# A two-layer cross-attention kernel: its start reordered, and the context of later batches loaded in 32 by 32 blocks and turned by VectorE

## The chip, the cores and the metric

The kernel runs on one core of one Trainium2 chip. The metric is device time in microseconds (us) of one execution. Everything is float32. The engines are named as in the profile: PE is TensorE (matmul), PEld its weight loads, DVE is VectorE, ACT is ScalarE, POOL is GpSimd, SP is the engine that issues nearly all DMAs.

## The reference, cut to what matters

There are 4 batches; x has 1024 rows of 512, the context 1024 rows of 384.

```python
# layer 0, 16 heads of 64
h = layernorm(x, gamma, beta)
Q, K, V = h @ Wq, context @ Wk, context @ Wv            # each 1024 x 1024 per batch
attn = softmax(Q K^T) * 64 ** -0.5
x = x + (attn @ V) @ Wo + bo
# layer 1, 16 heads of 32
xn = x * rsqrt(mean(x * x) + eps) * norm_w
q = xn @ wq;  k, v = split(context @ wkv)
q, k = rotate(q), rotate(k)                              # rotary position
q, k = q / |q|, k / |k|
attn = softmax(q k^T * sqrt(32))
out = x + (attn @ v) @ wout
```

Both layers multiply the context with weights along its 384 features. A matmul of PE contracts over partitions, so the kernel needs the context turned over: features in partitions, rows along the free axis.

## The kernel before, in words

**Stages.** The batches run one after the other, and each has three stages. Attention 0 works through 8 pairs of heads in 8 steps each (`Attention0.step`): scores on PE (L453), the negated maximum on DVE (L478), the exponential on ACT (L479), scaling on POOL (L484), a 32 by 32 block turn on DVE (L487), and 16 DMAs for every two steps that regroup the blocks (L498, tile eT), after which PE multiplies with the values (L514). Between the attentions the second layer's first queries and keys are made. Attention 1 has two halves (8 heads each) of 32 steps (`Attention1.step`): a block is one group of 4 heads and 256 queries, with four steps of key tiles, kk = 0 to 3. A step has 32 score matmuls (L692), two exponentials of 128x1024 (L702), the product with the values of the step before (L741), filling work, and additions on DVE that collect the sums of the exponentials (L711, L713, L715). The buffer of the exponentials, e, has two places (kk % 2), so the exponentials of a step wait until the additions and the product of the step two before have read theirs. Once a block PE multiplies the sums with ones (L775), and DVE inverts and divides (L760 to L768).

**Filling work.** All other work is cut into units, pairs of a cost and a function. `Units.fill(us)` is called once a step and issues units from the front of the list while it owes time; a unit of cost 0 is issued along with its neighbours. So the order of the list is the order in which the instructions enter the engines' queues, and every engine works strictly through its own queue. SP does so as well: it runs ahead of the others until a DMA must wait for its destination to be free, and all DMAs behind it then wait too. During the second half of attention 1 the units are the beginning of the next batch (`prepare_units(b + 1)`, `order(adds)`): weights and context loaded, context turned, x rows loaded, their mean and variance taken on DVE (`norms[h]["stats"]`, L251 and L252), normalised on DVE (`apply`, L268), turned on PE (`turn`, L283), and keys, queries and values of the first two pairs projected (L172). Among them lie the output additions of the batch that ends (`other`, two matmuls of PE and one addition of DVE, L332, for each of 8 tiles).

**The context.** `context_units` loads 8 tiles of 128 rows (L217), and turns them on PE: for each half of the rows and each 128 features, four 128x128 transposes into one PSUM bank (L226, tile ptc), then a copy by ACT (L144) into the turned context ctxT (cT in the profile). The row tiles have four buffers, ctxT has one, which lives from here to the last projection of values in the first half of attention 1.

**The start of batch 0.** The same units in an order of their own: `loads` names the DMAs in their order on SP, `first` is issued before the first step of attention 0, `rest` is handed out over its first steps.

**PSUM.** Scores have two tiles of two banks; four banks (in attention 1 three) serve everything else through `bank` and `free`.

Of the kernel before, what the change touches and what calls it, by code (L numbers as in the profile page):

```python
# [38 lines left out]
P = 128  # L39
# [69 lines left out]
def xattn_kernel(ctx: ExitStack, tc: tile.TileContext, a: dict, out: bass.AP):  # L109
# [28 lines left out]
    def free(pp, late=0.5):  # L138

        which["reads"] += 1  # L140
        read[held.pop(id(pp))[1]] = work.clock + late + 1e-6 * which["reads"]

    def evac(dst, src):
        nc.scalar.copy(dst, src)  # L144


    ident = const.tile([P, P], F32, name="ident")
    make_identity(nc, ident)
    ones = const.tile([P, HD1], F32, name="ones")
# [57 lines left out]
    def context_units(b, ct):  # L207

        raws = {}

        def load(h):
            for t in range(4 * h, 4 * h + 4):
                if b == 0 and h:
                    raws[t] = sb.tile([P, S], F32, tag="vals", bufs=4, name=f"c_{b}_{t}")[:, :DC]
                else:
                    raws[t] = sb.tile([P, DC], F32, tag="row", bufs=4, name=f"c_{b}_{t}")
                nc.sync.dma_start(raws[t], c[b, t * P : (t + 1) * P, :])  # L217

        def turn_over(h, k):
            if k == 0:  # L220
                if h == 0:
                    both = sb.tile([P, NC_, S], F32, tag="ctxT", bufs=1, name=f"cT_{b}")
                    ct.extend([both[:, :, :512], both[:, :, 512:]])
            pp = bank(f"ptc_{b}_{h}_{k}")
            for t in range(4):
                nc.tensor.transpose(pp[:, t * P : (t + 1) * P], raws[4 * h + t][:, k * P : (k + 1) * P], ident)  # L226
            evac(ct[h][:, k, :], pp)
            free(pp)

        return [  # L230
            {
                "load": [(0.0, lambda h=h: load(h))],
                "turn": [(0.45, lambda h=h, k=k: turn_over(h, k)) for k in range(NC_)],
            }
            for h in range(2)
        ]
# [424 lines left out]
    class Attention1:  # L661
# [17 lines left out]
        def step(self, half, g, qb, kk, kT, qT, v, o, us):  # L679
            n = f"{self.b}_{half}_{g}_{qb}_{kk}"  # L680
            self.n += kk == 0
            if kk == 1:
                self.add_up()
            if kk == 2 and self.late is not None:
                self.late(False)
            sc = [score(f"s1_{n}_{u}", (P, 2, 2, WQ)) for u in range(2)]
            for c in range(2):
                for j in range(4):
                    rr = slice(j * HD1, (j + 1) * HD1)
                    k = 2 * kk + c  # L690
                    for part in range(0, P, HD0):
                        nc.tensor.matmul(  # L692
                            sc[j // 2][part : part + HD0, j % 2, c, :],
                            kT[rr, g, k * P + part : k * P + part + HD0],
                            qT[rr, g, qb * WQ : (qb + 1) * WQ],
                            start=True,
                            stop=True,
                        )
            es = []
            for u in range(2):  # L700
                e = self.e[:, kk % 2, u]
                nc.scalar.activation(e, sc[u], AF.Exp, scale=float(np.sqrt(np.float32(HD1))))  # L702
                es.append(e)
            self.finish()
            self.last = (half, g, qb, kk, v, es, o, self.n % 2, self.lone)
            self.u.fill(us)

            acc, end = self.both[:, self.n % 2], self.both[:, 3]
            into = acc if kk == 0 else end if kk == NT // 2 - 1 else self.both[:, 2]
            for u in range(2):  # L710
                nc.vector.tensor_add(into[:, 2 * u : 2 * u + 2, :], es[u][:, :, 0, :], es[u][:, :, 1, :])  # L711
            if 0 < kk < NT // 2 - 1:
                nc.vector.tensor_add(acc, acc, into)  # L713
            if kk == NT // 2 - 1 and self.lone:
                nc.vector.tensor_add(acc, acc, end)  # L715
# [101 lines left out]
    def flat(lists):  # L817
        return [u for lst in lists for u in lst]

    def prepare_units(b):  # L820
# [4 lines left out]
        def load(names="kqv"):  # L825
            w[0] = pair_load(b, 0, names, w.get(0))
# [22 lines left out]

        st["project"] = lambda p: flat(project(p).values())  # L850
        st["rows"] = begin_rows_of
        cts = context_units(b, st["ct"])
        norms = norm_units(b, 0, st["hT"], load_rows(b))

        def order(other):

            pairs = [project(p) for p in range(2)]
            turned = [join(*norms[h]["turn"][:2]) + join(*norms[h]["turn"][2:]) for h in range(2)]
            n = len(other)

            def some(i):
                return flat(other[n * i // 6 : n * (i + 1) // 6])

            if b == 0:
                loads = [[(0.0, lambda: load("k"))], cts[0]["load"], cts[1]["load"], norms[0]["load"]]
                loads += [[(0.0, columns_load), (0.0, lambda: load("qv"))]]
                loads += [norms[1]["load"], pairs[0]["begin"], [(0.0, constants_load)]]
                first = cts[0]["turn"] + norms[0]["stats"] + pairs[0]["k"][:NC_] + norms[0]["apply"]
                first += cts[1]["turn"] + pairs[0]["k"][NC_:] + norms[1]["stats"]
                first += norms[0]["turn"] + pairs[0]["q"][:NQ] + norms[1]["apply"]  # L870
                rest = pairs[0]["v"][:4] + norms[1]["turn"] + pairs[0]["v"][4:] + pairs[0]["q"][NQ:]
                later = flat([pairs[1][c] for c in ("begin", "k", "q", "v")])
                return flat(loads) + first, rest, later
            return flat(
                [
                    [(0.0, load)] + cts[0]["load"] + some(0) + join(*cts[0]["turn"][:2]) + cts[0]["turn"][2:],
                    cts[1]["load"] + some(1) + join(*cts[1]["turn"][:2]) + cts[1]["turn"][2:],
                    norms[0]["load"] + some(2) + norms[0]["stats"] + pairs[0]["begin"] + pairs[0]["k"],
                    norms[0]["apply"] + some(3) + turned[0],
                    norms[1]["load"] + pairs[0]["v"] + norms[1]["stats"] + some(4),  # L880
                    norms[1]["apply"] + some(5) + turned[1] + pairs[0]["q"],
                    pairs[1]["begin"] + pairs[1]["k"] + pairs[1]["q"],
                ]
            ), pairs[1]["v"]
# [18 lines left out]
    for b in range(B):  # L903
# [14 lines left out]
        for p in range(NPAIR):  # L918
            later = 17.3 * (p == 0)
            other = []  # L920
            if p in by_rows:
# [258 lines left out]
```

## Time and profile before

| | |
|---|---|
| time, median of 3 runs | 2797.65 us (2794.89 to 2800.26) |
| the profiled execution, own time | 2795.07 us |
| its span, first to last instruction | 2793.1 us |
| PE busy | 2771.9 us (99%) |
| DVE busy | 2202.7 us (79%) |
| ACT busy | 1436.9 us (51%) |
| POOL busy | 952.9 us (34%) |
| DMA | 349.90 MB in 177616 packets |
| PE transposes of context (ptc) | 96 in all, 24 a batch |
| ACT copies into cT | 24, median 608 ns |

The profile is that of one execution; times in it are counted from the first instruction of the span. The 2.0 us around the span belong to the execution's time. A row of a group or of the order of time names start, length, engine, line, operation, output and input tiles, shapes, the number of instructions, and in brackets how long the engine was idle before and what ended that. A busy PE is not PE at its peak, since matmuls are pipelined and their ends are modelled.

### The profile page before, as it was taken

To read this page: it belongs to the slowest core of one execution; us is meant where nothing else is said; L and a number is where in the kernel's file an instruction comes from. 1 tells how busy PE (TensorE), PEld (TensorE's weight loads), DVE (VectorE), ACT (ScalarE), POOL (GpSimd) and SP (SyncE) were. 2 spreads that over 40 slices of the span, in tenths; PEclk is the share of its full clock that TensorE was granted. 3 is DMA by queue.
4 is the path that set the end of the run, shared out by engine and by line. 5 is a ranking of instruction groups with operands and counts; after the bars stand their busy time and mean duration, and the time that the engine had idled before them with its cause. 6 is when DMAs were issued, how large, how long until landed. Compare 5 with 4: busy or idle time off the path is not lost.

```text
span 2793.1 us, 82844 instructions
## 1 busy us (share of the span) xinstructions
PE 2771.9 (99%) x35344; PEld 1388.0 (50%) x35344; DVE 2202.7 (79%) x3140; ACT 1436.9 (51%) x2323; POOL 952.9 (34%) x776
## 2 busy tenths in 40 slices
PE   9999999999999999999999999999999999999999
PEld 4444445555444444554554444455445444445543
DVE  5677786888777778698877777869887777886987
ACT  4444443766544444476654444446664444444665
POOL 2343354430234335442023433444202343443410
PEclk9999999999999999999999999999999999999999
DMA  5788776010388877601048888750104887774000
GB/s 143 176 197 189 184 167 165 24 38 27 74 206 193 191 187 164 148 23 38 27 96 202 196 188 189 158 133 24 38 27 116 203 195 185 184 162 117 3 3 32
DMA packets 177616, 349.90 MB, mean 125 GB/s; under 512 B 37600, under 2 KB 93152, under 8 KB 177248
## 3 DMA queue, kind: packets, MB, share of 16 engines
q1 hardware_dynamic: 176848, 344.42, 51.9%
q8 instruction: 278, 4.55, 0.7%
q14 instruction: 90, 0.74, 0.1%
q10 hardware_dynamic: 400, 0.20, 0.0%
HBM read 67.64 MB, written 8.39 MB: 27 GB/s over the span
## 4 chain that ended last, share of the span: by engine, by line
PE 79%; DVE 2%; ACT 2%; issue 1%; POOL 1%; SPq 1%; DMA 0%; DVEq 0%; ACTq 0%
PE s L453 13%; PE av L514 13%; PE s L692 9%; PE av L741 8%; PE pv L172 7%; PE po L172 6%; PE pqT L194 4%; PE po L194 4%; PE q_p L172 4%; PE pkT L194 3%; PE k_p L172 3%; PE pqT L172 1%; PE pkT L172 1%; ACT e L702 1%; PE pth L283 1%
## 5 line engine op out<-in xcount | busy, mean ns | idle before, releaser
L478 DVE TENSOR_REDUCE m<-s 128x1 f32<-128x1024 f32 x512 | 602.9, 1220 | 357.0 <-PE s L453 354.0
L702 ACT ACTIVATE e<-s 128x1024 f32<-128x1024 f32 x512 | 496.8, 1022 | 279.1 <-PE s L692 274.3
L479 ACT ACTIVATE e<-s,m 128x1024 f32<-128x1024 f32 x256 | 283.1, 1110 | 465.2 <-DVE m L478 274.0
L484 POOL TENSOR_SCALAR raw<-raw,li 128x1024 f32<-128x1024 f32 x256 | 287.2, 1122 | 685.1 <-DVE li L483 677.2
L453 PE MATMUL s<-qk 64*64 64x512 f32 x4096 | 514.7, 598 | 2.2 <-ACT e L479 0.9
L479 ACT ACTIVATE raw<-s,m 128x1024 f32<-128x1024 f32 x256 | 285.4, 1115 | 367.5 <-DVE m L478 364.3
L514 PE MATMUL av<-eT,v 128*64 128x256 f32 x4096 | 470.1, 382 | 0.5 <-DMA eT<-e 0.5
L484 POOL TENSOR_SCALAR e<-e,li 128x1024 f32<-128x1024 f32 x256 | 287.4, 1124 | 472.5 <-DVE li L483 270.2
L514 PEld LDWEIGHTS av<-eT,v 128*64 128x64 f32 x4096 | 284.2, 137 | 227.6 <-issue 63.9
L711 DVE TENSOR_TENSOR both<-e 128x512 f32<-128x512 f32 x512 | 342.5, 698 | 67.1 <-ACT e L702 64.4
L487 DVE STREAM_TRANSPOSE e<-e 128x1024 f32<-128x1024 f32 x256 | 310.0, 1229 | 0.3
L487 DVE STREAM_TRANSPOSE e<-raw 128x1024 f32<-128x1024 f32 x256 | 309.9, 1228 | 0.0
L692 PE MATMUL s<-q,k 32*64 32x256 f32 x8192 | 299.2, 387 | 3.9 <-ACT e L702 2.6
L453 PEld LDWEIGHTS s<-qk 64*64 64x64 f32 x4096 | 151.2, 132 | 252.6 <-issue 198.0
L692 PEld LDWEIGHTS s<-q,k 32*64 32x64 f32 x8192 | 156.4, 131 | 158.0 <-ACT e L702 72.4
L172 PE MATMUL pv<-wv,cT 128*64 128x128 f32 (+1 forms) x3360 | 189.1, 273 | 1.4 <-ACT k L590 1.4
L172 PEld LDWEIGHTS pv<-wv,cT 128*64 128x64 f32 (+1 forms) x3360 | 173.8, 132 | 31.1 <-issue 14.6
L194 PE MATMUL pqT<-hT,w 64*64 64x512 f32 x1408 | 161.0, 589 | 0.0
L713 DVE TENSOR_TENSOR both<-both 128x1024 f32<-128x1024 f32 x128 | 156.8, 1225 | 4.4
L741 PE MATMUL av<-e,v 128*32 128x256 f32 x2048 | 137.1, 385 | 0.0
L741 PE MATMUL av<-e,rest 128*32 128x256 f32 x2048 | 136.9, 385 | 0.0
L332 DVE TENSOR_TENSOR x<-x,po 128x512 f32<-128x512 f32 x112 | 74.9, 680 | 67.5 <-PE po L172 67.4
(101 smaller groups left out, 3084.7 us busy)
## 6 DMA issues: line engine op xcount, KB each, us to landing
eT<-e SPq DMA_DIRECT2D x2048, 128.0 KB, 2.4
xr<-in_x_dram SPq DMA_DIRECT2D x32, 256.0 KB, 4.0
w<-in_Wq_dram SPq DMA_DIRECT2D x32, 256.0 KB, 3.2
x<-in_x_dram SPq DMA_DIRECT2D x32, 256.0 KB, 2.9
wo<-in_Wo_dram SPq DMA_DIRECT2D x16, 512.0 KB, 4.3
out_dram<-x SPq DMA_DIRECT2D x32, 256.0 KB, 2.5
c<-in_ctx_dram SPq DMA_DIRECT2D x32, 192.0 KB, 3.7
wv<-in_Wv_dram SPq DMA_DIRECT2D x32, 192.0 KB, 3.4
```

The lines of the kernel that those rows point to most:

```text
L172: nc.tensor.matmul(o[rr], lhsT[:, rr], rhs, start=start, stop=stop)
L194: nc.tensor.matmul(o["pp"][cc], o["lhsT"](k)[rr, cc], o["rhs"](k)[rr], start=first and k == 0, stop=not first and k == n - 1,)
L453: nc.tensor.matmul(sc[j][part : part + HD0, kb * 512 : (kb + 1) * 512], pr["qT"][r[j], i * P + part : i * P + part + HD0], pr["kT"][r[j], ...
L478: nc.vector.tensor_reduce(m[:, j : j + 1], sc[j], AX.X, ALU.max, negate=True)
L479: nc.scalar.activation(e[j], sc[j].rearrange("p (g s) -> p g s", g=4), AF.Exp, bias=m[:, j : j + 1], accum_out=l[:, j : j + 1])
L484: nc.gpsimd.tensor_scalar(e[j], e[j], li[:, j : j + 1], HD0**-0.5, ALU.mult, ALU.mult)
L487: self.turn = [lambda j=j: nc.vector.transpose(self.e[:, :, i % BQ * 2 + j, :], e[j]) for j in range(2)]
L514: nc.tensor.matmul(av[r[j], :W].rearrange("p (t a i) -> p t a i", t=BQ, a=4), pr["v"][:, k, r[j]], eT[:, j, :, :, k * 32 : (k + 1) * 32], ...
L692: nc.tensor.matmul(sc[j // 2][part : part + HD0, j % 2, c, :], kT[rr, g, k * P + part : k * P + part + HD0], qT[rr, g, qb * WQ : (qb + 1) ...
L702: nc.scalar.activation(e, sc[u], AF.Exp, scale=float(np.sqrt(np.float32(HD1))))
L711: nc.vector.tensor_add(into[:, 2 * u : 2 * u + 2, :], es[u][:, :, 0, :], es[u][:, :, 1, :])
L741: nc.tensor.matmul(self.av[rr, 0, :], v[g][:, 2 * kk + c, rr], es[j // 2][:, j % 2, c, :], start=first and c == 0, stop=end and c == 1,)
```

## The change

1. Six matmuls on a tile of zeros are issued at the very start, before any data is there.
2. In batch 0 the context is turned tile by tile (three transposes for each arriving tile, into three banks at once) instead of by features. The second half of its tiles uses a score tile for two of its banks. The loads, the values and the second half's turns are reordered.
3. In batches 1 to 3 PE no longer turns the context. Twelve DMAs load it straight into ctxT, each for 32 features of one group of 128: the piece of 32 rows by 32 features that belongs at partitions g*32 and columns n*32 is written there unturned, in runs of 32 numbers (128 bytes). DVE then turns the 32 by 32 blocks in place, in six instructions of 128x512, which stand between the output additions, the statistics and the normalisation of the next batch. All output additions come ahead of the first projection.
4. The two first additions of a step, one for each exponential, become one of twice the size, except in the last step of a block in the very last half.
5. In batch 0 two projections of values move from the end of attention 0 to pair 2.

```diff
+    still = const.tile([P, P], F32, name="still")
+    nc.vector.memset(still, 0.0)
+    idle = bank("idle")
+    for _ in range(6):
+        nc.tensor.matmul(idle[:, :P], still, still, start=True, stop=True)
+    free(idle)
...
+        def turn_tile(t):
+            h = t // 4
...
+            for k in range(NC_):
+                nc.tensor.transpose(wide[h][k][:, t % 4 * P : (t % 4 + 1) * P], raws[t][:, k * P : (k + 1) * P], ident)
+            if t % 4 == 3:
+                for k, pp in enumerate(wide[h]):
+                    evac(ct[h][:, k, :], pp)
...
+    def context_blocks(b, ct):
+
+        def load():
+            both = sb.tile([P, NC_, S], F32, tag="ctxT", bufs=1, name=f"cT_{b}")
+            ct.extend([both[:, :, :512], both[:, :, 512:]])
+            rows = c[b].rearrange("(n i) (k g f) -> k g i n f", i=32, g=4, f=32)
+            for k in range(NC_):
+                for g in range(4):
+                    to = both[32 * g : 32 * (g + 1), k].rearrange("p (n f) -> p n f", f=32)
+                    nc.sync.dma_start(to, rows[k, g])
+
+        def turn_over(h, k):
+            nc.vector.transpose(ct[h][:, k, :], ct[h][:, k, :])
...
-            for u in range(2):
-                nc.vector.tensor_add(into[:, 2 * u : 2 * u + 2, :], es[u][:, :, 0, :], es[u][:, :, 1, :])
+            both = self.e[:, kk % 2].rearrange("p u j c q -> p (u j) c q")
+            if self.lone or kk < NT // 2 - 1:
+                nc.vector.tensor_add(into, both[:, :, 0, :], both[:, :, 1, :])
...
-        cts = context_units(b, st["ct"])
+        cts = context_units(b, st["ct"]) if b == 0 else context_blocks(b, st["ct"])
...
             if b == 0:
-                loads = [[(0.0, lambda: load("k"))], cts[0]["load"], cts[1]["load"], norms[0]["load"]]
-                loads += [[(0.0, columns_load), (0.0, lambda: load("qv"))]]
+                loads = [[(0.0, lambda: load("k"))], cts[0]["load"], cts[1]["load"], [(0.0, lambda: load("v"))]]
+                loads += [norms[0]["load"], [(0.0, lambda: load("q")), (0.0, columns_load)]]
                 loads += [norms[1]["load"], pairs[0]["begin"], [(0.0, constants_load)]]
-                first = cts[0]["turn"] + norms[0]["stats"] + pairs[0]["k"][:NC_] + norms[0]["apply"]
-                first += cts[1]["turn"] + pairs[0]["k"][NC_:] + norms[1]["stats"]
+                c0, c1 = cts[0]["tiles"], cts[1]["tiles"]
+                first = c0 + norms[0]["stats"] + c1[:1] + pairs[0]["k"][:NC_] + norms[0]["apply"]
+                first += c1[1:] + pairs[0]["v"][:4] + pairs[0]["k"][NC_:] + norms[1]["stats"]
                 first += norms[0]["turn"] + pairs[0]["q"][:NQ] + norms[1]["apply"]
-                rest = pairs[0]["v"][:4] + norms[1]["turn"] + pairs[0]["v"][4:] + pairs[0]["q"][NQ:]
+                first += pairs[0]["v"][4:6] + norms[1]["turn"]
+                rest = pairs[0]["v"][6:] + pairs[0]["q"][NQ:]
...
+            turns = cts[0]["turn"] + cts[1]["turn"]
             return flat(
                 [
-                    [(0.0, load)] + cts[0]["load"] + some(0) + join(*cts[0]["turn"][:2]) + cts[0]["turn"][2:],
-                    cts[1]["load"] + some(1) + join(*cts[1]["turn"][:2]) + cts[1]["turn"][2:],
-                    norms[0]["load"] + some(2) + norms[0]["stats"] + pairs[0]["begin"] + pairs[0]["k"],
-                    norms[0]["apply"] + some(3) + turned[0],
-                    norms[1]["load"] + pairs[0]["v"] + norms[1]["stats"] + some(4),
-                    norms[1]["apply"] + some(5) + turned[1] + pairs[0]["q"],
+                    [(0.0, load)] + cts[0]["load"] + norms[0]["load"],
+                    flat(other[:3]) + turns[:1] + other[3] + norms[0]["stats"] + other[4] + turns[1:2],
+                    other[5] + turns[2:3] + other[6] + turns[3:4] + norms[0]["apply"] + other[7] + turns[4:],
+                    pairs[0]["begin"] + pairs[0]["k"] + turned[0],
+                    norms[1]["load"] + pairs[0]["v"][:4] + norms[1]["stats"] + pairs[0]["v"][4:],
+                    norms[1]["apply"] + turned[1][:1] + pairs[0]["q"][:NQ] + turned[1][1:] + pairs[0]["q"][NQ:],
                     pairs[1]["begin"] + pairs[1]["k"] + pairs[1]["q"],
                 ]
             ), pairs[1]["v"]
...
-                several = [4, 4, 2, 2] if p == 0 else [0, 0, 2, 2] if b == 0 and p == 2 else [2, 2, 2, 2]
+                several = [4, 4, 2, 2] if p == 0 else [0, 2, 2, 2] if b == 0 and p == 2 else [2, 2, 2, 2]
```

More of the change, by code (lines that the diff above doesn't have):

```diff
@@ L228, in turn_over @@
             free(pp)
+        wide = {}
+        def turn_tile(t):
+            h = t // 4
+            if t == 0:
+                both = sb.tile([P, NC_, S], F32, tag="ctxT", bufs=1, name=f"cT_{b}")
+                ct.extend([both[:, :, :512], both[:, :, 512:]])
+                wide[0] = [bank(f"ptc_{b}_0_{k}") for k in range(NC_)]
+            elif t == 4:
+                two = score(f"ptc_{b}_1")
+                wide[1] = [two[:, :512], two[:, 512:], bank(f"ptc_{b}_1_2")]
+            for k in range(NC_):
[3 more added lines that the diff above has]
+                    evac(ct[h][:, k, :], pp)
+                    if id(pp) in held:
+                        free(pp)
         return [
@@ L233, in context_units @@
                 "turn": [(0.45, lambda h=h, k=k: turn_over(h, k)) for k in range(NC_)],
+                "tiles": [(0.33, lambda t=t: turn_tile(t)) for t in range(4 * h, 4 * h + 4)],
+            }
+            for h in range(2)
+        ]
+    def context_blocks(b, ct):
+        def load():
+            both = sb.tile([P, NC_, S], F32, tag="ctxT", bufs=1, name=f"cT_{b}")
+            ct.extend([both[:, :, :512], both[:, :, 512:]])
+            rows = c[b].rearrange("(n i) (k g f) -> k g i n f", i=32, g=4, f=32)
[5 more added lines that the diff above has]
+            nc.vector.transpose(ct[h][:, k, :], ct[h][:, k, :])
+        return [
+            {
+                "load": [(0.0, load)] if h == 0 else [],
+                "turn": [(0.0, lambda h=h, k=k: turn_over(h, k)) for k in range(NC_)],
             }
@@ L709, in step @@
             into = acc if kk == 0 else end if kk == NT // 2 - 1 else self.both[:, 2]
-            for u in range(2):
-                nc.vector.tensor_add(into[:, 2 * u : 2 * u + 2, :], es[u][:, :, 0, :], es[u][:, :, 1, :])
+            both = self.e[:, kk % 2].rearrange("p u j c q -> p (u j) c q")
+            if self.lone or kk < NT // 2 - 1:
+                nc.vector.tensor_add(into, both[:, :, 0, :], both[:, :, 1, :])
+            else:
+                for u in range(2):
+                    part = slice(2 * u, 2 * u + 2)
+                    nc.vector.tensor_add(into[:, part], both[:, part, 0, :], both[:, part, 1, :])
             if 0 < kk < NT // 2 - 1:
@@ L858, in order @@
             turned = [join(*norms[h]["turn"][:2]) + join(*norms[h]["turn"][2:]) for h in range(2)]
-            n = len(other)
-            def some(i):
-                return flat(other[n * i // 6 : n * (i + 1) // 6])
             if b == 0:
-                loads = [[(0.0, lambda: load("k"))], cts[0]["load"], cts[1]["load"], norms[0]["load"]]
-                loads += [[(0.0, columns_load), (0.0, lambda: load("qv"))]]
+                loads = [[(0.0, lambda: load("k"))], cts[0]["load"], cts[1]["load"], [(0.0, lambda: load("v"))]]
```

## The prediction

> **What bounds the kernel now.** I read the page's busy shares first.
>
> ```profile
> PE 2771.9 (99%) x35344; PEld 1388.0 (50%) x35344; DVE 2202.7 (79%) x3140; ACT 1436.9 (51%) x2323; POOL 952.9 (34%) x776
> ```
>
> TensorE (PE) has work for all but 21.2 us of the 2793.1 us span, so time is won by taking work off PE or filling its few gaps, and lost wherever PE is made to wait. Next, the longest waits of PE itself (total us, times, longest):
>
> ```profile
> PE ptc L226 <- DMA c<-in_ctx_dram: 4.8, 3, 3.9
> ...
> PE sum L775 <- DVE both L715: 1.3, 3, 0.4
> ```
>
> The first is the start of the run, the second the end of a batch, where PE needs VectorE's (DVE's) last addition. Now the stretches the change touches: PE, PEld, DVE, ACT, POOL busy us, then clock, DMA share and GB/s. The first two rows are the start (the first scores begin at 22.44); the other five are the second half of batch 0's second attention, in which the next batch's context is turned.
>
> ```profile
> 0.00:9.40 9.40, 4.59 (x16) 2.79 (x18) 0.15 (x1) 3.04 (x4) 0.81 (x8) 1.00 0.82 264
> 9.40:22.44 13.04, 12.35 (x69) 5.43 (x65) 9.90 (x24) 6.09 (x10) 2.43 (x4) 1.00 0.73 232
> ```
>
> ```profile
> 601.60:717.00 115.40, 115.35 (x2129) 55.74 (x2132) 93.57 (x149) 77.99 (x98) 3.08 (x4) 1.00 0.13 39
> 601.60:611.00 9.40, 9.35 (x165) 4.75 (x172) 6.90 (x12) 6.91 (x11) 0.00 (x0) 1.00 0.14 44
> 611.00:621.00 10.00, 10.00 (x180) 4.92 (x172) 5.98 (x9) 7.75 (x10) 0.00 (x0) 1.00 0.42 132
> 621.00:631.00 10.00, 10.00 (x188) 4.39 (x182) 9.38 (x20) 4.95 (x6) 0.00 (x0) 1.00 0.27 83
> 631.00:641.00 10.00, 10.00 (x180) 4.14 (x176) 9.83 (x18) 6.35 (x8) 1.87 (x2) 1.00 0.01 2
> ```
>
> PE is full there, but DVE is nearly so from 621 to 641. Last, the order of time (start, length, engine, line): the transposes of context at the start and in that stretch, and what PE does right after them.
>
> ```profile
> 6.21 2.18 PE L226 MATMUL ptc<-ident,c 128*128 128x128 f32 x9 [0.29 <-DMA c<-in_ctx_dram]
> ...
> 12.02 1.53 PE L226 MATMUL ptc<-ident,c 128*128 128x128 f32 x12
> ```
>
> ```profile
> 607.40 1.53 PE L226 MATMUL ptc<-ident,c 128*128 128x128 f32 x12
> ...
> 608.98 1.07 PE L172 MATMUL po<-wo,o 128*32 128x512 f32 x8
> ...
> 615.58 1.53 PE L226 MATMUL ptc<-ident,c 128*128 128x128 f32 x12
> ...
> 617.04 0.66 PEld L692 LDWEIGHTS s<-q,k 32*64 32x64 f32 x32 [0.17 <-ACT cT L144]
> ```
>
> **Part 1, the start.** Until 22.44 us PE is idle 5.5 us (22.44 less 4.59 and 12.35), and its early work is slow: nine transposes in 2.18 us are 0.24 each, twelve later ones in 1.53 are 0.13. The change runs six matmuls on zeros ahead of the first context tile (3.92), turns the context tile by tile as it lands, and puts values and the second half's turns before the first scores. Laid out by the rows: first-half keys at about 7.7 instead of 8.3, and at full pace; then nine transposes (1.2), four values (2.84 for 48 matmuls at 24.31) and the second-half keys (2.79) end at 17.3 without a gap. The normalised rows are ready at 16.75: the wv load is moved ahead of the x rows and shifts the statistics (9.25 before) by 0.8 us for its 192 KB. Turns (2.0) and queries (3.6) end at 22.9, two more values and the other turns (3.6) at 26.4, where the scores start. Before, the same work plus step 0's scores (1.9) was done at 30.82, the start of step 1's; after, at 28.3: **-2.5 us**. If the zeros do not quicken the early matmuls it is -1.7; if the statistics come later still, -1; if the x rows come no later, -4. The work that leaves steps 0 to 15 lowers PE's load there from about 7.5 to 7.1 us a step, above DVE's 5.1 (two maxima of 1.18, two turns of 1.22), so nothing else takes over.
>
> The row says 0.24 at 6.2 and 0.13 at 12. [...] The profile's granted clock shows 1.00 throughout and so cannot decide.
>
> **Part 2, context of batches 1 to 3.** Removed per batch: 24 transposes. By the next PE row they hold PE from 607.40 to 608.98 and from 615.58 to 617.04, 3.0 us together: **-9.1** for three batches. Six ACT copies of 0.6 go too, worth nothing by themselves: ACT is 78 of 115 us busy.
>
> Added: six DVE turns of 128x512. A 128x1024 turn takes 1.23, a 128x256 one 0.44, so 0.70 each and 4.2 per batch. Also, all eight output additions (L332, 0.68) now fall in the first nine steps, where before only four did (605.5, 613.5, 621.0, 624.7): 2.7 more. From 601.6 to 641 DVE was busy 32.1 us; 4.2 and 2.7 more, less ten merged additions (0.65), make 38.4 us of work in a stretch that PE would now do in 36.4, and DVE cannot start on it at once (some 3.4 us of waiting for po and exp at its front remain). Walking DVE's queue in order, the first addition of the ninth step (scores at 630.9) ends at 641.7. It holds one of the two exponent buffers, so the exp two steps on, wanted at 639.1, is 2.6 us late; PE's step (3.77) is 0.7 longer than scores and exp (3.1) and takes that up. With 0.3 at the next step PE loses about 2 us per batch: **+6**. Bounds: 0 (more of DVE's front waiting is used) to +5 a batch (none of the slack is there).
>
> **The loads.** Eight rows of 1.5 KB packets become 12 DMAs of 1024 packets of 128 B, which write straight into ctxT. That tile is single, so SP must hold them until the last value matmul of the first half (600.7), whereas before the context was fetched early. Queued behind them on SP, and in the same rings, are the four x rows for statistics. What does a 128 B packet cost? The nearest row is the weights' 512 B packets, here alone in 692 to 698:
>
> ```profile
> DMA packets 1329, 0.67 MB, mean 112 GB/s; under 512 B 48, under 2 KB 1328, under 8 KB 1328
> ...
> q1 hardware_dynamic: 1328, 0.66, 37.9%
> ```
>
> 0.379 x 16 engines x 6 us / 1328 = 27 ns a packet. In the packet records 16 B ones took 9 ns, 512 B 27, 1 KB 46, 2 KB 84: a line of 8 ns plus 0.037 ns a byte, which gives 12.7 at 128 B. Against it: the 4 KB packets of eT, which like the blocks write into 32 partitions at a time, took 290 on average, 1.8 times the line, which would make 17. Bounds 9 and 27; I take 17, nearer to the line's end as the sizes on both sides lie on it. With 768 packets per engine that is 13.1 us, and 0.2 a DMA (the three weight DMAs spread over 2.7 us, not 2.16) makes 15.4: from about 601.5 to 616.9. The x rows follow, the first usable 1.8 us later, 618.7. DVE reaches the statistics at 620.4 (behind step 4's output addition), and the first turn at 616.6, when its four DMAs have been in for 8 us. So **0**, with 1.7 us of cover. Issue is no limit: 12 at the 0.59 of an eT issue are 7.1 us. The other loads that move on SP (pair 1's weights, from 618.6 to about 631) are not read before 690: 0.
>
> [...]
>
> **Part 3, the first addition.** Two additions of 0.65 become one of 1.225: 0.065 less DVE work in 256 steps, about 16 us off an engine that is not the bound. In the first halves (DVE 103.6 of 116.6 busy) I take **-1** for all, bounds 0 and -3. Against it: the single one starts only when both exps are done. At a batch's end the pair ran 720.50 and 721.42, then L715 at 722.15, then PE's sum at 723.43 after 0.4 of waiting; merged, all that ends 0.5 later: **+1.5** for three batches, at least 0. The last half keeps the pair at its last steps. Two values moved from pair 6 to pair 2 of batch 0 are PE work in either place: 0.
>
> **Sum.** -2.5 - 9.1 + 6 + 0 - 1 + 1.5 = -5.1 on the profiled execution's 2795.07 us (span 2793.1 and 2.0 around it), which lay 2.6 under the median of 2797.65: forecast 2792.5. A measurement of this kernel can tell about 0.2%, 5.6 us, from no change; the forecast stands just inside, so its case is split between faster and same.
>
> **Rivals.**
> *DVE keeps up.* The 93.6 of 115.4 us over the whole half leave 22 idle; if the queue runs late without reaching the exps, the +6 goes: -11.1, 2786.5. For it: the whole list is only 2 us longer than its time. Against: 9.83 of 10 busy already at 631 to 641.
> *The blocks land late (slower).* DVE works in order: if the x rows are not there at 620.4, the statistics stand and every addition behind them, then the exps, then PE. With 27 ns the blocks take 23.0 and end at 624.5, x rows at 626.3: 5.9 us of standing, with the 2 of slack already spent. Per batch 5.9 + 2 - 3.0 + 0.5 = 5.4; three are 16; with -3.5 for the rest +12.6: 2810. It begins at 19 ns and makes the change worthless from 21.5. For it: the 1.8 of the 4 KB packets. Against: the 9 ns.
> *The turns and output additions cost more* (bound +5 a batch): +15 for +6, sum +4, 2801.6.
>
> **How the numbers follow.** Forecast 0.45 (faster 0.2, same 0.24, slower 0.01); DVE keeps up 0.18 (all but 0.01 faster); late blocks 0.30 (slower 0.28, same 0.02); costlier queue 0.07 (same 0.02, slower 0.05). Together faster 0.37, same 0.29, slower 0.34. The forecast's own range is 2788 to 2798. The 8-in-10 range goes down to 2785 (DVE keeps up, and -4 at the start) and up to 2814 (late blocks at 27 ns, and +5 a batch on part of the queue); above it lies a block cost beyond every row.
>
> **What would show it.** Right: scores first at about 26.4 us, no PE wait for c beyond 3.9; no ptc after batch 0; six transposes of 0.70 on cT per batch; blocks landed by 617 and no DVE wait on xr; a few waits of exp on DVE additions totalling 2 us per batch. Wrong: DVE idle before st or cT with a DMA as releaser, DMA share near 0.9 for 20 us from 601, or steps of over 4 us from 620 to 650.

## The result, and the profile after

The changed kernel is slower: median 2803.64 us (2800.55 to 2810.03, 14 runs) against 2795.97 us (2794.34 to 2800.26, 14 runs) for the kernel before on the same chip, a ratio of 1.0027 (95% interval 1.002 to 1.0035), or +7.7 us. The forecast was 2792.5. The profiled execution of the changed kernel took 2805.74 us (span 2804.0); it lay 2 us above its median and that of the kernel before 1 us under, so differences between the two traces (10.9 us in the spans) overstate the medians' by some 3 us.

The busy shares of the page say little: PE has 3.7 us more of busy time for 60 instructions fewer, DVE 10 us less.

```profile
PE 2775.6 (99%) x35284; PEld 1384.2 (49%) x35284; DVE 2192.3 (78%) x2911; ACT 1427.9 (51%) x2305; POOL 980.5 (35%) x776
```

PE's own waits (total us, times, longest) say more. The 3.9 us for the first context tile are gone (0.9 is left, behind the zeros' 1.0). Two waits are new: turns of the normalised rows (pth) for DVE's normalisation (xr), three times, and pth for ACT's copy of the keys (k), four times. Two grew: exponentials 3.1 for 2.6, the batch's last sums 2.3 for 1.3.

```profile
PE pth L332 <- DVE xr L317: 5.5, 3, 1.8
PE pth L332 <- ACT k L639: 3.2, 4, 0.8
PE s L741 <- ACT e L751: 3.1, 9, 1.1
PE sum L829 <- DVE both L769: 2.3, 3, 0.8
...
PE ptc L249 <- DMA c<-in_ctx_dram: 0.9, 2, 0.7
```

To see where the time goes I took the start of every stage from the first score matmul of each in the trace, and subtracted the kernel before. The table gives what each stage took more or less (us) than before in the profiled execution of this and of the kernels told of below. "Start" ends at pair 2 of batch 0's first attention. "Rest" is all else, nearly all of it first attention; it came out at 0.4 to 3.0 in every kernel, also where nothing there differs (0.9 in `start_only`), at 2.6 and 0.4 in two executions of the same kernel (`late_and_pair` and `late_and_pair_again`), and is taken as scatter between executions.

| kernel | start | first half, each of 4 | second half of batch 0, 1, 2 | last half | rest |
|---|---|---|---|---|---|
| changed | -3.3 | +0.9 | +1.1, +2.5, +3.7 | +2.2 | +1.2 |
| `start_only` | -2.9 | 0.0 | 0.0, 0.0, 0.0 | 0.0 | +0.9 |
| `merge_only` | +1.5 | +0.9 | +0.5, +0.5, +0.5 | +0.5 | +2.5 |
| `pair_add` | -2.5 | 0.0 | 0.0, +1.6, +1.6 | 0.0 | +1.7 |
| `zeros_gap` | -1.7 | +0.9 | +1.1, +1.1, +1.1 | +0.6 | +3.0 |
| `order_late` | +0.4 | +0.9 | -0.8, -0.8, -0.8 | +2.3 | +2.0 |
| `late_and_pair` | -3.8 | 0.0 | -1.2, -1.2, -1.2 | 0.0 | +2.6 |
| `spread_and_pair` | -3.4 | 0.0 | -0.5, -0.5, -0.5 | 0.0 | +1.6 |
| `turns_apart` | -3.3 | 0.0 | -2.3, -2.3, -2.3 | 0.0 | +0.8 |
| `turns_apart_2` | -3.4 | 0.0 | -1.9, -1.9, -1.9 | 0.0 | +2.1 |
| `late_and_pair_again` | -3.6 | 0.0 | -1.2, -1.2, -1.2 | 0.0 | +0.4 |
| `no_zeros` | -1.2 | 0.0 | -1.2, -1.2, -1.2 | 0.0 | +3.0 |
| `blocks_32_bytes` | -1.3 | +0.9 | +25.5, +24.5, +25.1 | +0.5 | +0.5 |

**The start.** In the order of time, the zeros run from 1.04 (the trace lists the six as 12), the first twelve key matmuls take 2.80 where they took 3.77, and the scores begin at 25.44 (predicted 26.4).

```profile
1.04 2.93 PE L151 MATMUL idle<-still 128*128 128x128 f32 x12 [1.04 <-DVE still L148]
...
7.55 2.80 PE L179 MATMUL pkT<-cT,w 128*64 128x512 f32 x12
...
25.44 1.95 PE L502 MATMUL s<-qk 64*64 64x512 f32 x16
```

**The loads.** The twelve block DMAs are issued from 598.53 to 608.92, the x rows follow, and DVE reaches the statistics at 617.90 with no wait in brackets.

```profile
598.53 10.39 SPq L274 DMA_DIRECT2D cT<-in_ctx_dram  x12
609.02 2.00 SPq L359 DMA_DIRECT2D xr<-in_x_dram  x4
...
614.26 0.70 DVE L277 STREAM_TRANSPOSE cT<-cT 128x512 f32<-128x512 f32 x1
...
617.90 0.69 DVE L300 BATCH_NORM_STATS2 st<-xr 128x6 f32<-128x512 f32 x1
```

In the packets of 598.4 to 609, 81.2% of 16 engines for 10.6 us over 10680 packets is 12.9 ns a packet (taken as 17, with 12.7 by the line of sizes).

```profile
DMA packets 10681, 1.36 MB, mean 129 GB/s; under 512 B 10680, under 2 KB 10680, under 8 KB 10680
...
q1 hardware_dynamic: 10680, 1.35, 81.2%
```

**The second half.** The first row is the half of batch 0 as a whole, the second the stretch where DVE is at its limit (as at 631 to 641 before), the third a later one (columns as in the prediction).

```profile
601.00:717.00 116.00, 113.69 (x2088) 53.53 (x2087) 92.77 (x124) 74.03 (x89) 4.16 (x4) 1.00 0.18 43
629.00:639.00 10.00, 10.00 (x188) 4.45 (x188) 9.86 (x16) 5.13 (x6) 0.00 (x0) 1.00 0.01 2
659.00:669.00 10.00, 7.79 (x198) 5.19 (x183) 9.72 (x20) 5.19 (x8) 2.08 (x2) 1.00 0.02 3
```

PE stays full in the crowd that the prediction was about, and loses 2.2 us at 659 to 669, of which it said nothing. By the starts of its steps, counted from 0, the half is 1.3 us ahead of before at step 17 (662.0), and that one step then takes 7.9, 8.3 and 8.9 us in the three batches instead of 4.4. Up to there PE has been idle for 0.1 us, so the 1.3 is work and not waiting: 24 transposes fewer (3.0), 48 value matmuls not yet made (1.5), 24 matmuls of output additions made earlier (3.2). The order of time shows what step 17 meets:

```profile
663.95 1.49 PE L179 MATMUL pv<-wv,cT 128*32 128x128 f32 x48
...
665.37 1.01 POOL L211 TENSOR_TENSOR rs<-ve,nhalf 128x4 f32<-128x4 f32 x1
...
666.68 1.91 DVE L317 TENSOR_SCALAR xr<-xr,mv,rs 128x512 f32<-128x512 f32 x4
667.27 2.13 PE L332 MATMUL pth<-ident,xr 128*128 128x128 f32 x8 [1.82 <-DVE xr L317]
```

The second half of the next x rows is normalised at 666.68, when its statistics, POOL's reciprocal root and the divide of a block are through. PE has nothing left that comes before the turns of these rows: it stands 1.82 us, and then each pair of turns waits for its tile (2.13 for eight, which took 1.09 at 642.77 before). Gap and turns cost 2.9 us (1.82, and 2.13 less 1.09). In the kernel before the normalisation came at 666.07, in a half that began 2.2 us later, but output additions were still in the list there:

```profile
664.53 1.04 PE L172 MATMUL po<-wo,o 128*32 128x512 f32 x8
...
666.07 1.91 DVE L268 TENSOR_SCALAR xr<-xr,mv,rs 128x512 f32<-128x512 f32 x4
...
667.65 1.90 PE L172 MATMUL po<-wo,o 128*32 128x512 f32 x16
```

The change has put all eight of them ahead of the first projection.

**The clock.** Batches 1 and 2 lose more than batch 0 at the same place with the same instructions. Three stretches and the rest of batch 1's second half (the column before the DMA share is the granted clock):

```profile
1355.00:1363.00 8.00, 5.79 (x149) 3.95 (x139) 7.76 (x19) 4.01 (x7) 2.08 (x2) 1.00 0.01 2
1363.00:1367.00 4.00, 4.00 (x53) 1.72 (x56) 2.11 (x2) 1.88 (x3) 0.00 (x0) 0.57 0.00 0
1367.00:1418.40 51.40, 50.64 (x872) 21.78 (x864) 35.48 (x39) 33.28 (x40) 0.00 (x0) 1.00 0.07 20
```

Right behind the gap the clock falls to a half, for 3.4 us here (0.50 from 1363.48 to 1366.89), 6.8 in batch 2 (0.50 from 2056.38), and not at all in batch 0; another 3.4 us lie in the last half, at 2704.9. This is no matter of one execution: the mean clock is under 1 in 13 of the 14 of this kernel, and in none of the kernel before on the other chips.

### The profile page after: what moved, and what is told of

Its sections match the earlier page's. It is cut to its first block, busy times and chain, and to the rows that moved or that the text cites. A ratio compares the mean times of both kernels' runs of the same rounds, so it can differ in the third digit from the quotient of the medians.

```text
span 2804.0 us, 82501 instructions
## 1 busy us (share of the span) xinstructions
PE 2775.6 (99%) x35284; PEld 1384.2 (49%) x35284; DVE 2192.3 (78%) x2911; ACT 1427.9 (51%) x2305; POOL 980.5 (35%) x776
## 4 chain that ended last, share of the span: by engine, by line
PE 90%; DVE 5%; ACT 2%; issue 1%; POOL 1%; DMA 1%; SPq 0%; DVEq 0%; ACTq 0%
PE s L502 17%; PE av L563 15%; PE s L741 9%; PE pv L179 8%; PE av L795 7%; PE po L179 6%; PE pqT L201 5%; PE po L201 5%; PE pkT L201 4%; PE q_p L179 4%; PE k_p L179 3%; PE pqT L179 2%; PE pkT L179 2%; DVE m L527 1%; ACT e L751 1%
## 5 line engine op out<-in xcount | busy, mean ns | idle before, releaser
L761 DVE TENSOR_TENSOR both<-e 128x1024 f32<-128x1024 f32 x248 | 305.0, 1231 | 103.3 <-ACT e L751 101.6
L767 DVE TENSOR_TENSOR both<-both 128x1024 f32<-128x1024 f32 x128 | 162.6, 1271 | 4.4
L179 PE MATMUL q_p<-wq,hT 128*32 128x256 f32 (+1 forms) x1920 | 126.1, 379 | 0.0
```

The lines of the kernel that those rows point to most:

```text
L179: nc.tensor.matmul(o[rr], lhsT[:, rr], rhs, start=start, stop=stop)
L761: nc.vector.tensor_add(into, both[:, :, 0, :], both[:, :, 1, :])
```

## The experiments

Medians, each with the kernel before on the same chip:

| kernel | median us (runs) | before | difference | ratio, 95% |
|---|---|---|---|---|
| `start_only` | 2792.92 (11) | 2796.62 | -3.7 | 0.9989 (0.998 to 0.9998) |
| `pair_add` | 2797.28 (11) | 2796.62 | +0.7 | 1.0002 (0.9994 to 1.0011) |
| `order_late` | 2796.91 (11) | 2796.62 | +0.3 | 1.0003 (0.9994 to 1.0011) |
| `zeros_gap` | 2802.07 (9) | 2796.62 | +5.5 | 1.0021 (1.0011 to 1.0031) |
| `merge_only` | 2803.74 (8) | 2796.41 | +7.3 | 1.0026 (1.0016 to 1.0036) |
| `late_and_pair` | 2789.65 (8) | 2796.41 | -6.8 | 0.9976 (0.9965 to 0.9986) |
| `spread_and_pair` | 2791.58 (11) | 2796.41 | -4.8 | 0.9986 (0.9977 to 0.9995) |
| `turns_apart` | 2786.14 (5) | 2796.12 | -10.0 | 0.9966 (0.9952 to 0.9979) |
| `turns_apart_2` | 2787.26 (6) | 2796.12 | -8.9 | 0.997 (0.9958 to 0.9981) |
| `late_and_pair_again` | 2789.46 (9) | 2796.12 | -6.7 | 0.9977 (0.9967 to 0.9986) |
| `no_zeros` | 2791.05 (11) | 2796.12 | -5.1 | 0.9984 (0.9975 to 0.9992) |

### pair_add: the first addition as two again

```diff
-            both = self.e[:, kk % 2].rearrange("p u j c q -> p (u j) c q")
-            if self.lone or kk < NT // 2 - 1:
-                nc.vector.tensor_add(into, both[:, :, 0, :], both[:, :, 1, :])
...
+            for u in range(2):
+                nc.vector.tensor_add(into[:, 2 * u : 2 * u + 2, :], es[u][:, :, 0, :], es[u][:, :, 1, :])
```

> The changed kernel with its first additions as a pair again. Theory A (the single addition frees both exponent places later, so the exponentials two steps on start late, and the last addition of a batch ends later): each of the four first halves gets its 0.9 us back, each batch's end 0.4, the last half 0.5 and perhaps the 1.7 of a halved clock: -5 to -7 us against the changed kernel, about 2797 to 2799. The 1.8 us wait of pth on xr in each second half stays. Rival B (the first halves lose their 0.9 us to something else, the single addition only takes work off DVE): the first halves stay 0.9 longer than before, time 0 to +1 us.

The 0.9 of each first half and the 2.2 of the last half are gone, and with them the pth wait on k. The wait at step 17 stays, a little shorter, and in batches 1 and 2 the clock is halved for 3.4 us behind it (mean clock 0.999 in this execution), which is their +1.6 (batch 0 has 0.0):

```profile
PE pth L332 <- DVE xr L317: 4.1, 3, 1.4
```

So the merged addition, which the forecast counted at +0.5 in all, makes nearly all of the 7.7 us: 7.0 by the two differences to the kernel before (7.7 less 0.7). Of the 2.2 in the last half, 0.5 is there in `merge_only` and `zeros_gap` too; the other 1.6 is the stretch of halved clock. What is left of the change ends level with the kernel before.

### order_late: two output additions back behind the later projections

```diff
-                    other[5] + turns[2:3] + other[6] + turns[3:4] + norms[0]["apply"] + other[7] + turns[4:],
+                    other[5] + turns[2:3] + turns[3:4] + norms[0]["apply"] + turns[4:],
...
-                    norms[1]["load"] + pairs[0]["v"][:4] + norms[1]["stats"] + pairs[0]["v"][4:],
-                    norms[1]["apply"] + turned[1][:1] + ...
+                    norms[1]["load"] + pairs[0]["v"][:4] + norms[1]["stats"] + pairs[0]["v"][4:] + other[6],
+                    norms[1]["apply"] + other[7] + turned[1][:1] + ...
```

> The changed kernel with the last two output additions (PE work of 3.4 us) put back between the second statistics and the turns of the second half's rows. Theory C (the second halves lose because PE reaches those turns before DVE has normalised, with no other PE work left in between, and the clock is then halved): the wait of pth on xr is gone, no stretch of halved clock in the second halves of batches 0 to 2, each of these halves 2.5 to 4.5 us shorter: -9 to -12 us against the changed kernel's profiled 2805.7, median about 2794. Rival D (DVE is overloaded by six turns and the stall only moves, as the prediction had it): the second halves stay longer than before by 1 us or more, with exp waiting on DVE additions elsewhere, -3 us at most.

The pth wait on xr is gone and each second half is 0.8 us shorter than before, 2.0 to 4.5 shorter than in the changed kernel. The expected median was missed by 3. One reason is a new wait near the tenth step: PE needs DVE's last addition of a block for the sums.

```profile
PE av L829 <- DVE both L769: 3.4, 3, 1.1
```

ACT is held at the same place:

```profile
640.23 1.94 ACT L751 ACTIVATE e<-s 128x1024 f32<-128x1024 f32 x2 [2.67 <-DVE both L761]
```

That is a lateness of DVE of the kind that the prediction described. In the changed kernel it cost PE nothing: there the normalisation of four rows (L317, 1.9 us) stands behind this addition (634.53 against 632.76), here, with two output additions fewer ahead of it, in front (635.93 against 640.17). (The table's start of +0.4 belongs to the profiled execution, which took 2800.70, 3.8 above this kernel's median; its first key matmuls were slow, see `no_zeros`.)

### zeros_gap: six matmuls on zeros in the gap

```diff
+                    norms[1]["apply"] + [(0.0, zeros)] + turned[1][:1] + ...
```

`zeros` is six matmuls of the tile `still` into a free bank, whose result nothing reads.

> The changed kernel with six matmuls on zeros put where PE waits for the second normalisation; their result is not used. Theory E (the wait itself costs about 2.9 us a batch and the halved clock after it is a separate price of 1.4 to 2.5 in those batches where it falls): pth still starts as late, but the clock stays whole in all second halves of batches 0 to 2, each about 1.1 us longer than before, as batch 0 was: about -4 us in the profiled execution, and the median -2 to -4. Rival F (the halved clock has nothing to do with this idle time): halved stretches at the same places, no change of time.

Most of PE's idle time is filled (0.4 of the 1.8 is left) without any useful work done earlier, and the second halves come out at +1.13, +1.14 and +1.13 where the changed kernel has +1.12, +2.47 and +3.65. No stretch of half clock is left in the trace (granted clock 1.00 at 1290 to 1420 and at 1980 to 2115), and 7 of 9 executions have a mean clock of 1.000, where 1 of 14 of the changed kernel has. So the spread between batches was the clock behind the gap. Without it a half is 1.1 longer than before, and 0.5 of this is the merged addition at the batch's end (`merge_only`). By the two differences to the kernel before the median is 2.2 under the changed kernel's, at the low end of what was expected; the two 95% intervals overlap.

### start_only: the kernel before with parts 1, 2 and 5 of the change

The context of batches 1 to 3, the order and the additions are those of the kernel before.

```diff
-        cts = context_units(b, st["ct"]) if b == 0 else context_blocks(b, st["ct"])
+        cts = context_units(b, st["ct"])
```

> The kernel before with nothing but the new start of batch 0 (zeros, tile by tile turns, values early, two values moved to pair 2); context of batches 1 to 3 turned on PE and additions in pairs as before. Theory G: the start is worth 3.3 us at pair 2 of batch 0, of which 3.0 are left at the first scores of attention 1: 2.8 to 3.3 us under the kernel before, no halved clock later. Rival H (what the start gains is handed back, as PE work is only moved): within 1 us of the kernel before.

-3.7 us by the medians, -2.9 by the trace at pair 2; every later stage in the table but "rest" equals the kernel before. So the reordered start does about what was predicted (-2.5), and the rest of the change must cost some 11 us (7.7 and 3.7).

### merge_only: the kernel before with the merged addition alone

```diff
-            for u in range(2):
-                nc.vector.tensor_add(into[:, 2 * u : 2 * u + 2, :], es[u][:, :, 0, :], es[u][:, :, 1, :])
+            both = self.e[:, kk % 2].rearrange("p u j c q -> p (u j) c q")
+            if self.lone or kk < NT // 2 - 1:
+                nc.vector.tensor_add(into, both[:, :, 0, :], both[:, :, 1, :])
...
```

> The kernel before with the single first addition alone. Theory A: +0.9 in each first half, +0.4 at each batch's end, +0.5 in the last half and 1.7 more if the clock is halved there: +4 to +7 us, 2800 to 2804. Rival B (as the prediction had it: 16 us less DVE work is worth -1, the later end +1.5): -1 to +1.5.

It is 7.3 us slower than the kernel before. By stages: 0.9 in each of four first halves, the same as in the changed kernel, 0.53 at each of three batch ends and 0.53 at step 5 of the last half, 5.7 together. The other 1.6 could not be placed; the interval of the 7.3 (4.5 to 10.1) allows for 5.7. ACT's waits in the first half of batch 0, before and with this edit alone:

```profile
ACT e L702 <- PE s L692: 34.8, 26, 2.3
```

```profile
ACT e L702 <- PE s L692: 29.6, 23, 2.3
...
ACT e L702 <- DVE both L712: 2.7, 2, 1.6
ACT e L702 <- DVE both L718: 1.9, 1, 1.9
ACT e L702 <- DVE o L773: 1.8, 1, 1.8
```

Before, an exponential was hardly ever held by anything but its scores; now DVE holds four of them. Step 6 of that half, first in the kernel before and then in the changed one:

```profile
506.50 1.12 PE L692 MATMUL s<-q,k 32*64 32x256 f32 x32
506.63 2.49 DVE L711 TENSOR_TENSOR both<-e 128x512 f32<-128x512 f32 x4
...
507.66 1.94 ACT L702 ACTIVATE e<-s 128x1024 f32<-128x1024 f32 x2 [0.81 <-PE s L692]
```

```profile
503.42 1.12 PE L741 MATMUL s<-q,k 32*64 32x256 f32 x32
504.01 2.35 DVE L761 TENSOR_TENSOR both<-e 128x1024 f32<-128x1024 f32 x2
...
505.32 1.94 ACT L751 ACTIVATE e<-s 128x1024 f32<-128x1024 f32 x2 [1.55 <-DVE both L761]
```

DVE has just normalised four tiles of the x rows and comes late to its additions. With two additions the first of 0.6 frees the place of the first exponential; with one, that place comes free only after the whole 1.2. The exponential starts 1.90 after its scores instead of 1.16. That 0.74 is the step's loss (+0.7 from step 6 to step 7), and it goes on to ACT's copy of the keys and PE's turn behind it.

### late_and_pair: order_late and pair_add together

> The changed kernel with both mendings: additions in pairs, and the last two output additions behind the second statistics. Theories A and C together: first halves and last half as before (0.0), no stretch of halved clock, PE's wait of 1.1 on the additions near the tenth step mostly gone; each second half with its batch end 1.5 to 2.5 us shorter than before, start 2 to 3: 2787 to 2790, faster than the kernel before by over 0.2%. Rival (the turns on DVE keep costing what PE saves): second halves as long as before, 2793 as with the start alone.

-6.8 us, a median in the expected range: the start, and 1.2 a half. A half was expected to gain 1.5 to 2.5 and the wait near the tenth step to be mostly gone; that missed, the wait stays:

```profile
PE av L824 <- DVE both L764: 3.6, 3, 1.2
```

In DVE's queue the normalisation stands ahead of the block's last addition:

```profile
631.09 1.88 DVE L317 TENSOR_SCALAR xr<-xr,mv,rs 128x512 f32<-128x512 f32 x4
...
635.38 1.23 DVE L764 TENSOR_TENSOR both<-both 128x1024 f32<-128x1024 f32 x1
```

### spread_and_pair: turns and output additions spread otherwise

```diff
-                    flat(other[:3]) + turns[:1] + other[3] + norms[0]["stats"] + other[4] + turns[1:2],
-                    other[5] + turns[2:3] + turns[3:4] + norms[0]["apply"] + turns[4:],
+                    flat(other[:2]) + turns[:1] + other[2] + turns[1:2] + norms[0]["stats"] + other[3],
+                    turns[2:3] + norms[0]["apply"] + other[4] + turns[3:],
...
+                    norms[1]["load"] + pairs[0]["v"][:4] + other[5] + norms[1]["stats"] + pairs[0]["v"][4:] + other[6],
```

> As late_and_pair, but with three output additions taken out of the first nine steps instead of two and the DVE turns earlier, so that DVE is less crowded while it turns. If what is left of the loss is DVE's crowd in these steps, each second half comes nearer to the full 3.0 us that PE is relieved of: 2.5 to 3.0, in all 2785 to 2787. If not, the same as late_and_pair.

A miss: 2791.58, and 0.5 a half instead of 1.2. The wait near the tenth step is gone, but DVE is late in the seventh to ninth step instead, and the exponentials are held more often:

```profile
PE s L741 <- ACT e L751: 6.0, 21, 0.6
```

Here, taking an output addition out of the front did not help; the turns, 0.7 each, moved into its place (three of them in a row at 626.50).

### blocks_32_bytes: the blocks in runs of 8 numbers

```diff
-            rows = c[b].rearrange("(n i) (k g f) -> k g i n f", i=32, g=4, f=32)
+            rows = c[b].rearrange("(n i) (k g u f) -> k g u i n f", i=32, g=4, u=4, f=8)
```

with four DMAs for each one of the change, 48 a batch. It asks whether the rival of the late blocks was real.

> The changed kernel with 48 block loads of 32-byte runs instead of 12 of 128 bytes: 3072 packets per DMA engine. The line of 8 ns plus 0.037 ns a byte gives 9.2 ns each, 28 us: blocks end near 628, x rows 630, 12 us after DVE wants them at 617.9. The prediction's rival mechanism (late rows stop DVE, DVE stops exp, exp stops PE): DVE waits on xr for 10 to 13 us, PE stands nearly as long less some 3 us of cover: +7 to +11 us in each of three batches, 2825 to 2838. If packets are limited otherwise (27 ns each): blocks end near 683 and each batch loses over 60 us.

One execution took 2873.28 us, far above the expected 2825 to 2838. The mechanism was the one named: DVE stands for the x rows behind the blocks, and the exponentials and PE behind it.

```profile
DVE st L301 <- DMA xr<-in_x_dram: 73.0, 7, 20.8
...
PE s L742 <- ACT e L752: 63.0, 12, 20.6
```

The size was off (DVE stood 20.8 where 10 to 13 were expected). A packet took 8.9 ns by the records, 27 us for the 3072 of an engine, but SP was at its issues for 37.14 us, whether by its own work or held back behind them:

```profile
600.60 37.14 SPq L275 DMA_DIRECT2D cT<-in_ctx_dram  x48
```

That is 0.77 a DMA of 1024 packets, against 0.87 for the 128 B ones (10.39 for 12). So the rival exists, and the change as made is far from it with its 12 DMAs and 768 packets per engine a batch.

### turns_apart and turns_apart_2: the turns between the keys, the normalisation behind them

```diff
-                    other[5] + turns[2:3] + turns[3:4] + norms[0]["apply"] + turns[4:],
-                    pairs[0]["begin"] + pairs[0]["k"] + turned[0],
+                    ... + norms[0]["stats"] + other[4] + turns[1:2] + other[5] + turns[2:3],
+                    pairs[0]["begin"] + pairs[0]["k"][:1] + turns[3:4] + pairs[0]["k"][1:2] + turns[4:5],
+                    pairs[0]["k"][2:3] + turns[5:] + norms[0]["apply"] + pairs[0]["k"][3:] + pairs[0]["v"][:2] + turned[0],
```

The first half's keys need only three of the six turns; the others are handed out between the keys. The rest is `late_and_pair`, with `other[6]` ahead of the second statistics. `turns_apart_2` puts `other[4]` behind `turns[1]`, `other[5]` behind the normalisation, and leaves all values behind `turned[0]`.

> late_and_pair with the DVE turns and the first normalisation spread further, between the key projections (a turn behind each of the first keys), and the second half's statistics later. If the 1.2 us that PE still waits for DVE's additions near the tenth step (3.6 in three batches) comes from turns and normalisation standing in a row in DVE's queue, that wait is gone and each second half is 0.8 to 1.3 us shorter than in late_and_pair: 2786 to 2787.5. If DVE has simply too much to do in these steps, the wait stays or moves: 2789 to 2790.

> As turns_apart, with one more output addition moved behind the first normalisation. Same two readings: 2786 to 2787.5, or 2789 to 2790.

`turns_apart` has the lowest median of this study: 10.0 us under the kernel before, 2.25 a half, and the wait near the tenth step is not in its list any more:

```profile
PE s L741 <- ACT e L751: 2.6, 9, 0.6
PE pv L179 <- ACT q L639: 1.9, 4, 0.5
PE ptc L249 <- DMA c<-in_ctx_dram: 1.1, 2, 0.8
```

The turns stand as they did in `late_and_pair`, in twos at 629.80 and 633.45. What moved is the normalisation: it now stands behind the block's last addition.

```profile
632.30 1.23 DVE L764 TENSOR_TENSOR both<-both 128x1024 f32<-128x1024 f32 x1
...
634.67 1.88 DVE L317 TENSOR_SCALAR xr<-xr,mv,rs 128x512 f32<-128x512 f32 x4
```

In the second one the normalisation is in front again (631.84, the addition at 634.95), and the wait stays:

```profile
PE av L824 <- DVE both L764: 2.9, 3, 1.0
```

Its median, 2787.26, lies in the first expected range all the same, with 1.9 a half. So the kernels with this wait (`order_late`, `late_and_pair`, `turns_apart_2`, `no_zeros`) have the normalisation just ahead of that addition; `turns_apart`, `pair_add` and the changed kernel, without the wait, have it behind. An edit that moves the normalisation alone was not run.

### no_zeros, with late_and_pair_again beside it

`no_zeros` is `late_and_pair` without the tile `still`, its memset and its six matmuls.

> late_and_pair unchanged, beside the other three on the same chip: 2789 to 2790.5.

> late_and_pair without the six matmuls on zeros. If they bring the full clock early (5 us in most profiles with them, 10 in the kernel before), the start loses 0.8 to 1.5 us without them: 2790.5 to 2791. If the clock's start is chance, no difference beyond the spread of single starts, 2789.5.

By the medians the zeros are worth 1.6 us (2791.05 less 2789.46), though the two kernels' single executions overlap. Without them the first transposes are slow again, and the key matmuls, 2.80 with zeros, take 4.23:

```profile
3.84 2.51 PE L242 MATMUL ptc<-ident,c 128*128 128x128 f32 x9 [3.84 <-DMA c<-in_ctx_dram]
...
8.30 4.23 PE L172 MATMUL pkT<-cT,w 128*64 128x512 f32 x12
```

The zeros do not bring the full pace every time. In the three profiled executions without zeros the keys took 3.71 to 4.23; with zeros 2.79 to 2.80 in eight of eleven, but 3.82, 4.04 and 5.13 in the others. The slowest is that of `order_late`:

```profile
9.00 5.13 PE L179 MATMUL pkT<-cT,w 128*64 128x512 f32 x12
```

## Why the prediction was wrong

**The sum.** By differences of medians, the start is -3.7 (`start_only`), the context as changed +4.4 (`pair_add` less `start_only`), the merged addition +7.0 (changed less `pair_add`); that they make up the +7.7 follows from how they were taken. By the stages of the traces the context costs 3.2 (`pair_add`: 0.0, 1.6, 1.6). By itself, in `merge_only`, the merged addition came out at +7.3. The forecast had -2.5, -3.1 and +0.5. The first term held; the others did not.

**Part 3, the first addition, is the term that failed most.** "-1 for all", with bounds 0 and -3, was worked out from DVE's busy time alone: less work on an engine that is crowded in the first halves. The sentence "the single one starts only when both exps are done" was applied at a batch's end, where +1.5 was right (0.53 three times, and once more in the last half). It was not applied to the release: the prediction itself said that an addition "holds one of the two exponent buffers", but only for the crowd of Part 2. The merged addition holds that place 0.6 us longer whenever DVE is behind, and in the first halves that costs 0.9 each (0.7 at step 6, 0.2 at step 14). Instead of +0.5 the runs showed 5.7 by stages and 7.0 to 7.3 by medians. The bound on the gain side was allowed, and none on the loss side.

**Part 2, the context: no cost where it was looked for, and one at a place that was not looked at.** The 9.1 us of transposes did go. The +6 for the crowd, "about 2 us per batch", did not come: up to step 17 the changed kernel's PE is idle for 0.1 us. DVE was full as forecast (9.86 of 10 us at 629 to 639), but the normalisation stood behind the block's last addition, and PE had the output additions to do. A lateness of DVE reached PE only in other orders of the list: 1.1 to 1.2 us a batch in `order_late` and `late_and_pair`; `turns_apart`, without it, gains 2.25 of the 3.0. What failed besides is the sentence that "all eight output additions now fall in the first nine steps": it priced what they add there (2.7 us of DVE) and not what they leave at the place they came from. They were PE's only filling work between the second statistics and the turns that wait for them. The gap and the slow turns cost 2.9 us, nearly the 3.0 of the transposes, and the halved clock 1.3 and 2.5 more in batches 1 and 2; PE's waits show it (5.5 us on xr). `order_late` removes that wait by putting two of the eight back. The rival of costlier turns and output additions forecast 2801.6, 2 us under the measured 2803.64, but by luck: it had Part 2 at +5.9 where +4.4 was measured, Part 3 at +0.5 where 7.0 was, and put its loss into the first ten steps, where PE was full.

**The loads were right.** Behind the start there is no DVE wait on xr, and the blocks landed by 611.3 instead of 617, since a packet took 12.9 ns and not 17. The line through the other sizes (12.7) was the better guide than the 4 KB packets of eT (1.8 times the whole line would have been 23; 17 comes out only if the part per byte alone grows). The issue took 10.39 and not 7.1, which cost nothing here, and a DVE turn the 0.70 that was estimated. `blocks_32_bytes` shows the rival's mechanism with its price, at a packet count that the change does not have.

**The start was right** in its working and nearly in size: -3.3 in the trace, and the key matmuls were at full pace (2.80) in the profiled execution. The prediction could not tell from the profile whether the zeros would quicken them: `no_zeros` answers it on average (1.6 us), and three slow starts with zeros show that it is not certain. The granted clock of 1.00 throughout that the prediction read was no measurement at the start: the clock records of that trace begin at 10.32 us, those of the changed kernel at 4.97.

**DVE keeps up** was the rival that `turns_apart` comes nearest to (-10.0 for its -11.1), in another order of the list and without the merged addition. What was to show the forecast wrong was put at 620 to 650; the long step was at 665, outside the stretch that was watched.

## What to carry to other kernels

Joining two instructions that each free a buffer saved a little work on one engine here (1.25 us for the pair at step 6, 1.18 for the one) and moved the first release back by half of the joint duration (0.6); price that wait wherever the engine comes late to the work, even when the joined work is less. When work is moved forward in a hand-ordered list, look at the place it leaves: here PE's filler between a slow chain (statistics, root, normalisation) and the matmul that waits for it was worth 2.0 to 4.5 us a batch, against 3.0 for the transposes removed. Read the new list once for each long chain of other engines, asking what PE still has to do while the chain runs.

## What the runs showed of the hardware that was not expected

- The granted clock fell to a half behind a gap in an otherwise full PE. In the changed kernel it fell behind PE's step 17 for 3.41 us in batch 1 and for 6.83 in batch 2 (0.50 in both), not in batch 0. The longest single idle time there was 1.82 us, within 8 us of which PE was busy for 5.79. With zeros in the gap it did not occur in the trace (1.00 in the second halves of batches 1 and 2 of `zeros_gap`).
- In the changed kernel's trace the clock's changes lie 3.413 us or multiples of it apart: it falls at 1363.48, 2056.38 and 2704.91 us, which are 203.0 and 190.0 times 3.413 apart, and the falls last one, two and one such time. Why it struck in some batches and not in others, no run here shows.
- A DMA of 1024 small packets kept SP, or the queue behind it, for 0.87 us at 128 B and 0.77 at 32 B (10.39 for 12, 37.14 for 48), so a quarter of the bytes per packet saved 0.10 us of it.
